# An RWKV block on one core: a small product moves into the duplicate column tile of another

## The chip, the cores and the metric

The kernel runs on one core of a Trainium2 chip. The metric is the device time of one execution in microseconds (us). Engines are named as in the profile: PE is TensorE, DVE is VectorE, ACT is ScalarE, POOL is GpSimd, SP issues most of the DMAs. All data is fp32.

## The reference

The inputs are 8 batches of 256 tokens with 512 channels (32 heads of 16). One batch goes through time mixing and channel mixing:

```
xn = layernorm(x);  sx = shift(xn) - xn
xxx = tanh((xn + sx*maa_x) @ maa_w1)            # 5 parts of 32
x5[g] = xn + sx*(maa_stack[g] + xxx[g] @ maa_w2[g])      # g = 0..4
w = exp(-exp(time_decay + tanh(x5[1] @ decay_w1) @ decay_w2))
r = x5[3] @ Wr.T;  k = x5[0] @ Wk.T;  v = x5[2] @ Wv.T;  g = silu(x5[4] @ Wg.T)
for each token:                                  # s: 16x16 for each head
    a = k (x) v
    out = r . (u*a + s)                          # u = faaaa
    s = a + w*s
x = x + (groupnorm(out) * g) @ Wo.T
xn2 = layernorm(x);  sx2 = shift(xn2) - xn2
x = x + sigmoid((xn2 + sx2*maa_r) @ Wr2.T) * (relu((xn2 + sx2*maa_k) @ Wk2.T)**2 @ Wv2.T)
```

The term `r . (u*a)` is a token's own part: for each head it is the sum over 16 channels of r*k*u, times v. The rest of `out`, `r . s`, is the scan's part.

## The kernel before

Every batch has three stages. `inputs_of_scan` makes the five mixtures x5, the decay w and the projections r, k, v, g. `scan` runs the recurrence: channels lie on partitions, time on the free axis, and for each of 16 pieces of a batch (4 blocks by 4) DVE multiplies by k (the line with `vs`, 128x1024), DVE scans (TENSOR_TENSOR_SCAN, `st`), POOL multiplies by r (`st<-st,r`), and PE gathers four such tiles into a PSUM tile `pat{b}_{blk}` (16 matmuls, 4 column tiles of 32). `rest` does the group norm, the gate, the product with Wo and the channel mixing.

The text names a piece of work by the name of the buffer that it fills, with the batch at the end or in the middle: `psd3` is the decay product of batch 3, `pc3` the own-part product of batch 3, `pat3_0` the gather of its block 0, `psx3` the product with maa_w1, `psm3_1_0` and `psm3_4_0` the products with maa_w2 (each fills four PSUM tiles at once). In the profile all tiles of one pool have one name: every PSUM tile of that pool is `ps`.

- **Decay product `psd`.** Its output has 128 partitions in four column tiles of 32. Tiles 0 and 1 are x5[1] @ decay_w1 (64 columns). Tile 2 is the fifth part of maa_w1, 32 columns, and tile 3 is the same 32 columns again: the array of maa_w1 holds them twice, so that a copy of 64 rows can be taken. ACT then writes tanh of it to `hd` (2 instructions of 64x256) and to `tb` (2 instructions of 64x256), the second four times over the partitions.
- **Own part `pc`.** In `scan`, POOL makes rk = r*k (two tiles of 128x512). PE multiplies it with `hm`, the head mask times faaaa: four matmuls of 256 columns, one in each column tile, into a PSUM tile of its own. ACT copies the sums to all heads' rows (4 copies of 64x256, back into rk). POOL multiplies by v (`att`). DVE later adds each `pat` to `att`, and only then the PSUM tile of that `pat` comes free.
- **Buffers.** PSUM has 8 banks; six are the pool `ps`, two are `wrep`, the expanded decay of a scan. Almost every product of PE needs a tile of `ps` that an ACT or DVE instruction has emptied.
- **Order.** Nothing in the code fixes the order across stages. Every piece of work is an `Op` with a rank out of the table `TURNS`. `Plan.order` always takes the piece with the lowest rank whose inputs are ready, gives it buffers, and sets its start by estimated durations; the pieces are then issued in the order of these starts, and each engine works through its own in order. Stages of three batches overlap: inputs of b+1 and b+2, scan of b, rest of b-1. `Plan.tiles` chooses for a product marked "any" between 128-column weights and four 32-column tiles, after its neighbours. `Plan.tables` puts in the ACT table loads.

Of the kernel before, what the change touches and what calls it, by code (L numbers as in the profile page):

```python
# [68 lines left out]
class Plan:  # L69
# [50 lines left out]
    def stage(self):  # L120
# [6 lines left out]
        677 802 765 774 803 804 821 805 860 824 852 838 1013 770 81 748 784 607 738 881 698 699 767 663 60 619  # L127
        756 91 643 714 124 757 469 782 729,
        30 129 83 79 695 150 166 545 703 460 225 541 73 316 365 644 421 350 761 593 558 731 697 742 665 716 606
        612 758 652 638 45 12 206 135 808 568 845 534 874 634 542 820 145 117 879 485 847 57 560 337 360 834 863  # L130
        781 484 160 48 214 892 822 937 723 271 65 565 897 722 557 100 910 523 945 148 15 134 906 1003 394 935 72
        588 660 954 5 823 944 277 379 562 766 844 9 709 576 976 459 1015 51 143 440 1009 177 1021 477 543 1030
        1052 676 1087,
        797 389 501 402 640 445 437 706 313 559 807 829 239 368 217 893 811 136 119 428 907 688 743 938 627 309
        953 395 29 966 506 848 609 1065 991 510 55 1058 531 299 335 1019 882 586 1026 312 1048 1034 854 888 505
        1000 328 940 696 569 305 372 508 655 653 996 311 259 59 215 154 26 1142 1157 371 1147 867 251 1089 388
        234 752 1088 374 1099 1105 1101 611 794 1094 587 1096 306 308 1053 629 1069 1166 383 1197 1102 273 673
        1146 483 1164 1143 439 1158 191 176 1135,
        826 658 646 426 347 228 900 862 288 626 877 668 38 220 3 977 876 227 231 419 980 983 744 672 997 367 258
        17 1079 675 1167 417 387 903 1185 885 455 615 1172 361 197 252 1168 210 232 331 667 1126 574 399 415  # L140
        1024 1132 650 1 1127 466 205 53 577 1129 662 90 1206 470 185 1232 349 1290 404 561 408 896 1255 359 620
        1229 329 1281 380 1085 423 598 1277 186 585 199 1223 970 1301 324 343 1204 1300 591 1324 1217 409 369
        1293 694 1405 246 528 1323 812 285 1358,
        1309 1265 800 507 911 128 1331 322 97 452 209 297 1365 1007 592 25 1109 1363 1035 656 33 1372 835 63
        1373 211 11 283 1410 537 1422 779 464 799 1431 456 1428 1120 1423 420 639 1477 1424 458 926 178 1447
        1453 1018 921 1203 595 1383 909 1540 1338 174 202 1068 1455 635 1121 836 245 1514 524 1513 310 1600 1344
        1605 1283 853 353 236 1595 1579 115 1345 270 1551 1212 1555 730 1549 1544 1113 1559 512 1416 366 188
        1517 1534 28 1611 1591 321 446 74 509 1492 1618 1023 1678 1601 614 1653,
        1408 1552 654 401 659 95 1473 1371 740 1604 1584 1012 1629 1478 1063 725 451 1631 1494 825 1590 1669 787
        1241 1657 196 1001 495 1682 1709 1729 818 1145 1734 1691 1711 1743 1244 1262 265 575 1738 1392 1014 1719  # L150
        334 1690 1587 597 1039 1038 1326 1421 1377 1548 1457 276 810 1716 1419 737 833 1715 429 1751 354 1760
        1562 1811 1834 1632 1836 949 1772 62 1783 1771 685 1776 161 1082 1803 1258 1493 1762 1286 1800 1327 1280
        1160 341 346 1766 573 54 1780 1795 444 1388 1812 1047 1861 1865 44 1918 67 481 1887,
        1761 518 496 669 631 405 1784 1139 988 1499 1785 390 1842 1348 552 333 162 702 1789 866 1849 1417 1123
        1866 1913 375 1010 318 1937 1961 1900 1173 1298 1978 1152 527 1844 1853 1955 1561 414 1980 975 624 1749
        223 1965 1304 1368 1420 1385 1979 1369 875 1036 1778 1315 832 1908 1261 1443 1097 2015 10 2028 279 2063
        1332 66 2075 1982 2061 1224 93 2008 2039 1948 139 2047 454 2090 2095 2086 1201 1731 2083 1634 2103 1230
        2172 465 138 2014 2084 301 2113 2041 250 2080 300 69 2050 2220 625 2251 2232 149 2257,
        1845 2029 972 427 1184 289 1846 1724 1075 2049 2046 599 2072 1321 1221 579 147 2074 948 116 291 2079 489
        1823 2088 472 1838 292 2112 623 2169 1017 1713 2142 2149 682 1896 1454 2144 1029 947 2163 2102 1895 2140  # L160
        1370 474 2121 1220 1710 1901 2126 1781 1933 1655 2122 887 1098 1585 2128 1723 549 1922 286 2193 212 2192
        636 2217 2227 2001 1464 1639 2162 533 2180 2177 841 2200 31 2210 2000 2105 1699 1998 2207 1091 1538 1756
        1234 323 590 2183 2209 327 2214 2161 233 2023 2230 457 2012 2328 771 2064 2353 2376 2391,
        1985 2093 1033 1395 1027 219 1869 1264 1874 2174 2153 789 2188 1532 1438 487 226 2194 2097 1880 2197
        2199 1912 1660 2233 1977 2032 648 2274 384 2280 412 2065 2256 2286 425 1111 2307 2279 1444 386 2298 2277
# [1017 lines left out]
```

## Time and profile before

| | |
|---|---|
| three runs | 619.63, 620.3, 623.63 us; median 620.3 |
| profiled execution | 621.16 us, its span 619.4 us |
| busy, share of the span | PE 97%, DVE 88%, POOL 86%, ACT 66% |
| granted TensorE clock | 0.999 of full speed |

The span runs from the first to the last instruction; 1.76 us of the profiled execution lie around it. A matmul in the profile is an instruction of half a product (fp32 takes two), and ends are modelled, so successive rows of PE overlap by about 0.2 us: how long PE is taken by a piece is read from the start of its row to the start of the next. On ACT, DVE and POOL the durations are the instructions' own.

### The profile page before, as it was taken

What the parts mean: (1) busy time and instruction counts of PE and PEld (TensorE: products, weight loads), DVE (VectorE), ACT (ScalarE), POOL (GpSimd) and SP (SyncE); (2) the same over time, 40 slices, a digit from 0 to 9 for tenths busy, and PEclk for the clock granted to TensorE, in tenths of its full rate; (3) what the DMA queues carried; (4) which work ended last, traced back from release to release, by engine and by line L of the source; (5) the groups of instructions that cost most, each with busy time, mean ns of one, the idle gap of its engine ahead of it and who ended that gap; (6) DMA issues with size and microseconds to landing.
All of it is one profiled execution on the core that took longest, in us unless ns stands there. A gap on an engine that the chain in (4) does not pass through costs nothing.

```text
span 619.4 us, 17893 instructions
## 1 busy us (share of the span) xinstructions
PE 602.7 (97%) x7490; PEld 342.6 (55%) x7490; DVE 545.3 (88%) x492; ACT 409.7 (66%) x962; POOL 534.4 (86%) x441
## 2 busy tenths in 40 slices
PE   9999999998999999999999999999999999999987
PEld 8665555546634764357453784465744464445454
DVE  5489999999999899898998989999999999995342
ACT  4796368668974788757786787766884387634531
POOL 2789999999999999988999989999997989798030
PEclk9999999999999999999999999999999999999999
DMA  8696766887789676958976695867876697951642
GB/s 286 223 232 166 187 182 172 241 240 201 200 202 258 159 203 180 264 152 236 276 204 207 194 236 155 235 193 204 220 208 192 167 278 206 249 192 51 194 133 83
DMA packets 52497, 124.81 MB, mean 202 GB/s; under 512 B 5696, under 2 KB 11200, under 8 KB 52416
## 3 DMA queue, kind: packets, MB, share of 16 engines
q1 hardware_dynamic: 48048, 119.41, 69.8%
q10 hardware_dynamic: 4368, 4.26, 2.3%
q8 instruction: 59, 0.97, 0.7%
q14 instruction: 22, 0.18, 0.1%
HBM read 115.26 MB, written 8.39 MB: 200 GB/s over the span
## 4 chain that ended last, share of the span: by engine, by line
PE 56%; POOL 15%; DVE 11%; DMA 7%; issue 5%; ACT 5%; ACTq 0%; DVEq 0%; POOLq 0%
PE ps L423 48%; POOL st L957 8%; DMA vs<-vo 5%; DVE st L954 5%; PE ps L965 5%; DVE vs L952 2%; POOL mix L692 2%; POOL mix L778 1%; PE ps L818 1%; PE ps L636 1%; DMA s<-in_state 1%; PE ps L547 1%; POOL vs L949 1%; POOL sx L664 1%; DMA vo<-v 1%
## 5 line engine op out<-in xcount | busy, mean ns | idle before, releaser
L954 DVE TENSOR_TENSOR_SCAN st<-wrep,vs 128x1024 f32<-128x1024 f32 x128 | 289.4, 2279 | 5.9 <-ACT wrep L936 2.6
L957 POOL TENSOR_TENSOR st<-st,r 128x1024 f32<-128x1024 f32 x128 | 254.2, 2004 | 9.6 <-DVE st L954 9.0
L952 DVE TENSOR_TENSOR vs<-vs,ps 128x1024 f32<-128x1024 f32 x122 | 144.2, 1205 | 2.4 <-ACT ps L935 1.9
L423 PE MATMUL ps<-Ws,mix 128*32 128x512 f32 (+3 forms) x872 | 115.7, 586 | 0.7 <-ACT mix L1041 0.7
L423 PEld LDWEIGHTS ps<-Ws,mix 128*32 128x32 f32 (+1 forms) x872 | 38.6, 117 | 64.2 <-issue 57.7
L692 POOL TENSOR_TENSOR mix<-mix,xn 128x512 f32<-128x512 f32 x44 | 48.0, 1103 | 26.0 <-ACT mix L690 24.6
L778 POOL TENSOR_TENSOR mix<-mix,xn 128x512 f32<-128x512 f32 x62 | 66.8, 1099 | 1.6 <-DVE mix L762 1.4
L965 PE MATMUL ps<-st,con 128*32 128x256 f32 x1024 | 61.8, 381 | 0.3 <-DVE x L1031 0.2
L423 PE MATMUL ps<-mix,Wv 128*32 128x256 f32 (+1 forms) x904 | 58.6, 380 | 1.2 <-DVE mix L775 1.1
L423 PE MATMUL ps<-mix,Ws 128*32 128x256 f32 (+1 forms) x736 | 58.0, 380 | 1.3 <-ACT mix L690 0.8
L423 PE MATMUL ps<-mix,Wg 128*32 128x256 f32 (+1 forms) x832 | 58.6, 380 | 0.7 <-POOL mix L806 0.7
L423 PE MATMUL ps<-mix,Wk 128*32 128x256 f32 (+1 forms) x712 | 58.2, 380 | 1.1 <-POOL mix L778 1.0
L423 PE MATMUL ps<-mix,Wr 128*32 128x256 f32 (+1 forms) x808 | 58.5, 380 | 0.0
L423 PE MATMUL ps<-Ws,g 128*32 128x512 f32 (+1 forms) x416 | 56.6, 592 | 0.6 <-DVE mix L801 0.6
L760 ACT ACTIVATE ps<-ps,vec 128x256 f32<-128x256 f32 x112 | 46.9, 445 | 10.8 <-PE ps L423 9.1
L423 PEld LDWEIGHTS ps<-mix,Ws 128*32 128x32 f32 (+1 forms) x736 | 38.6, 121 | 19.1 <-ACT mix L690 1.6
L423 PEld LDWEIGHTS ps<-mix,Wk 128*32 128x32 f32 (+1 forms) x712 | 39.0, 122 | 17.8 <-POOL mix L778 2.4
L423 PEld LDWEIGHTS ps<-mix,Wv 128*32 128x32 f32 (+1 forms) x904 | 35.0, 114 | 22.7 <-DVE mix L775 1.8
L423 PEld LDWEIGHTS ps<-mix,Wg 128*32 128x32 f32 (+1 forms) x832 | 36.5, 116 | 19.8 <-POOL mix L806 1.1
L423 PEld LDWEIGHTS ps<-mix,Wr 128*32 128x32 f32 (+1 forms) x808 | 37.0, 117 | 18.2 <-issue 1.0
L965 PEld LDWEIGHTS ps<-st,con 128*32 128x32 f32 x1024 | 31.6, 110 | 26.1 <-issue 4.7
L1107 ACT ACT_TABLE_LOAD x35 | 44.9, 1283 | 0.6
(134 smaller groups left out, 879.2 us busy)
## 6 DMA issues: line engine op xcount, KB each, us to landing
vs<-vo SPq DMA_DIRECT2D x128, 512.0 KB
Ws<-in_fk SPq DMA_DIRECT2D x16, 512.0 KB
Ws<-in_wo SPq DMA_DIRECT2D x16, 512.0 KB
Ws<-in_fr SPq DMA_DIRECT2D x16, 512.0 KB
Ws<-in_fv SPq DMA_DIRECT2D x16, 512.0 KB
x<-in_x SPq DMA_DIRECT2D x9, 512.0 KB
vo<-v ACTq DMA_DIRECT2D x32, 128.0 KB
out<-o SPq DMA_DIRECT2D x15, 256.0 KB
```

The source lines that it names most:

```text
L423: nc.tensor.matmul(out[i : i + n], lhsT=w[:, i : i + n], rhs=x, start=first, stop=final)
L547: nc.tensor.matmul(ps()[:, 0, :], lhsT=warm[:, 0, 0:P], rhs=warm[:, 0, 0:T], start=True, stop=True)
L636: nc.tensor.transpose(to[:, m, n * P : (n + 1) * P], xh[n]()[:, k * P : (k + 1) * P], idt())
L664: take(512, [sx], [xn], lambda xn=xn, sx=sx, e=nc.vector if quick else nc.gpsimd: e.tensor_tensor(sx(), xn()[:, :, 0:T], xn()[:, :, 1 : T ...
L692: gp(512, t, [t, xn[q]], lambda q=q, t=t: nc.gpsimd.tensor_tensor(t(), t(), xn[q]()[:, :, 1 : T + 1], ALU.add))
L760: act(256, p_, [p_, vec], lambda g=g, q=q, m=m, p_=p_: nc.scalar.activation(p_()[:, m, :], p_()[:, m, :], AF.Identity, bias=col(f"maa_{g}" ...
L778: gp(512, t, [t, xn[q]], lambda q=q, t=t: nc.gpsimd.tensor_tensor(t(), t(), xn[q]()[:, :, 1 : T + 1], ALU.add))
L952: dve(4 * T, [vs], [vs, kp], lambda vs=vs, kp=kp: nc.vector.tensor_tensor(paired(vs()), paired(vs()), doubled(kp()), ALU.mult))
L954: dve(4 * T, [st], [w, vs], lambda w=w, vs=vs, st=st: nc.vector.tensor_tensor_scan(st().rearrange("p n t -> p (n t)"), w().rearrange("p n ...
L957: gp(4 * T, st, [st, r], lambda st=st, r=r: nc.gpsimd.tensor_tensor(paired(st()), paired(st()), doubled(r()), ALU.mult), 1.815)
L965: nc.tensor.matmul(pat()[32 * g : 32 * g + 32, 0, :], lhsT=con()[:, s : s + 32], rhs=done[j]()[:, g, :], start=(j == 0), stop=(j == 3),)
L1107: nc.scalar.preload_act_table_set(op.table)
```

## The change

The second copy of the fifth part is no longer computed. For every batch b after the first, the decay product `psd{b}` computes tiles 0 to 2 as before, and in tile 3 (partitions 96 to 127) the own part's sums of batch b-1: `hm` times rk of b-1. The sums of channel blocks 0 and 1 go to the two halves of psd's own PSUM tile, those of blocks 2 and 3 to a second one, `pc{b-1}`. The product of `pc` by itself is gone for batches 0 to 6; batch 7 has no next batch and keeps it.

Since the sums now lie on 32 partitions, ACT copies them with 8 instructions of 32x256 in place of 4 of 64x256, and `tb` is written with 4 instructions of 32x256 in place of 2. Since psd{b} reads rk of batch b-1, the code of rk moves from `scan` to the end of `inputs_of_scan`, and the stages are written down in another sequence. `psd{b}` now waits for POOL's two rk of batch b-1, and `att` of batch b-1 for psd{b}. All numbers of `TURNS` are new.

```diff
-                    for i in range(0, P, 32):
+                    for i in range(0, P if b == 0 else 96, 32):
                         w, src = (dw1()[:, k, i : i + 32], x5[1]) if i < DEC else (w1()[:, k, P + i - DEC : P + i - 32], xin)
                         nc.tensor.matmul(
                             pd()[i : i + 32, 0, :], lhsT=w, rhs=src[k // 2]()[:, k % 2, :], start=(k == begin), stop=(k == end))
+                    if own:
+                        nc.tensor.matmul(own["pc"][k // 2]()[96:128, k % 2, :], lhsT=hm()[:, k, :],
+                                         rhs=own["rks"][k // 2]()[:, k % 2, :], start=True, stop=True)
...
+            if own:
+                own["pc"] = [pd, new("ps", f"pc{b - 1}")]
+                pe(0.432 * len(ks), own["pc"], [dw1, w1, hm, *ins, *own["rks"]], mm, "columns", [hd, tb])
+                continue
...
-        for rows in (slice(0, 64), slice(64, 128)):
-            act(345, tb, [pd], lambda rows=rows: nc.scalar.activation(tb()[rows, :], pd()[64:128, 0, :], AF.Tanh), "tanh")
+        n = 32 if own else 64
+        for rows in (slice(i, i + n) for i in range(0, P, n)):
+            act(345, tb, [pd], lambda rows=rows: nc.scalar.activation(tb()[rows, :], pd()[64 : 64 + n, 0, :], AF.Tanh), "tanh")
...
-        pe(0.437, [pc], [hm, *rks], mm, "columns")
-        for q in range(NQ):
-            for h in range(0, P, 64):
-                act(350, rks[q], [pc], lambda q=q, h=h: nc.scalar.copy(
-                    rks[q]()[h : h + 64, 0, :], pc()[64 * q : 64 * q + 64, 0, :]))
+        if b == NB - 1:
...
+        else:
+            for q, pc in enumerate(got["pc"]):
+                for h in range(0, P, 32):
+                    act(350, rks[q], [pc], lambda q=q, h=h, pc=pc: nc.scalar.copy(
+                        rks[q]()[h : h + 32, 0, :], pc()[96:128, h // 32 % 2, :]))
...
     TURNS = """
-        677 802 765 774 803 804 821 805 860 824 852 838 1013 770 81 748 784 607 738 881 698 699 767 663 60 619
```

The built programs have these counts: PE 400 pieces of work before and 393 now (the seven products), ACT 914 and 956 (28 more copies, 14 more tanh) with 35 and 31 table loads inside the kernel, DVE 490 and 490, POOL 429 and 429, DMAs 251 and 251 on SP and ACT together.

Three places follow, all around the own part of batch 3. Numbers behind names are those of buffers; lines are those of either program (L910 before is L831 now, L818 is L828, L423 is L432, L917 is L942, L826 is L844, L971 is L996).

PE before, at the own part of batch 3: ps_173 is `pv2`, the variance product of batch 2, ps_174 is `pc3`, ps_172 is `psfk1_1`, a product of the channel mixing of batch 1.

```order
L423 MATMUL ps_172<-mix_118,Ws_165 32x256 x8
L989 MATMUL ps_173<-sq_160,con 32x256 x2
L989 MATMUL ps_173<-sq_159,con 32x256 x2
L910 MATMUL ps_174<-rk_151,hm 32x256 x2
L910 MATMUL ps_174<-rk_152,hm 32x256 x2
L423 MATMUL ps_172<-mix_116,Ws_167 32x256 x8
```

PE now, at the decay product of batch 4: ps_173 is `psd4`, ps_174 is `pc3`, ps_170 ahead of it is a part of v of batch 4.

```order
L432 MATMUL ps_170<-mix_110,Wv_77 32x256 x8
L828 MATMUL ps_173<-mix_114,dw_69 32x256 x2
L828 MATMUL ps_173<-mix_117,mw_66 32x256
L831 MATMUL ps_173<-rk_152,hm 32x256
L828 MATMUL ps_173<-mix_114,dw_69 32x256 x2
L828 MATMUL ps_173<-mix_117,mw_66 32x256
L831 MATMUL ps_173<-rk_152,hm 32x256
L828 MATMUL ps_173<-mix_113,dw_69 32x256 x2
L828 MATMUL ps_173<-mix_119,mw_66 32x256
L831 MATMUL ps_174<-rk_151,hm 32x256
```

The four matmuls of the own part left their place between `pv2` and the channel mixing and stand one by one in the fourth position of each group of the decay product, with gather `pat3_0` far ahead of them and `pat3_1` four products behind.

ACT before, the copies of the own part of batch 3 out of ps_174.

```order
L1107 ACT_TABLE_LOAD
L992 ACTIVATE sq_160<-ps_173,eh 128x256
L917 COPY rk_152<-ps_174 64x256
L917 COPY rk_151<-ps_174 64x256 x2
L917 COPY rk_152<-ps_174 64x256
L1040 ACTIVATE mix_119<-ps_172 128x512
```

ACT now, what empties ps_173 (`psd4` with half of the own part).

```order
L956 DMA vo_144<-v_130 4x32x256
L942 COPY rk_152<-ps_173 32x256 x3
L844 ACTIVATE tb_122<-ps_173 32x256 x2
L942 COPY rk_152<-ps_173 32x256
L844 ACTIVATE tb_122<-ps_173 32x256 x2
L971 COPY vs_148<-s_82 128x4
L582 ACTIVATE xh_87,mv_91<-x_161 128x512
L841 ACTIVATE w_134<-ps_173 64x256 x2
```

ACT now, some rows later, what empties ps_174 (`pc3`, the other half).

```order
L971 COPY vs_147<-s_82 128x4
L942 COPY rk_151<-ps_174 32x256 x2
L867 COPY r_128<-ps_170 128x2x256
L942 COPY rk_151<-ps_174 32x256
L867 COPY r_126<-ps_171 128x2x256
L942 COPY rk_151<-ps_174 32x256
```

Four copies in a row became eight in two lots, among the tanh of the decay and the work of other batches.

DVE before, the first add of a gather of batch 3 (L971, ps_173 is `pat3_0`) among scans (L954) and mixtures (L762).

```order
L954 SCALAR_TENSOR_TENSOR st_153<-wrep_169,vs_146 128x1024
L971 TENSOR_TENSOR att_141<-ps_173,att_141 128x256
L762 TENSOR_TENSOR mix_107<-ps_170,sx_105 128x512
L762 TENSOR_TENSOR mix_111<-ps_175,sx_105 128x512
L954 SCALAR_TENSOR_TENSOR st_154<-wrep_169,vs_145 128x1024
```

DVE now: ps_175 is `pat3_0`, ps_170 is `pat3_1` (L979 are the scans, L977 the products with k, L1056 the residual of batch 2).

```order
L979 SCALAR_TENSOR_TENSOR st_158<-wrep_169,vs_147 128x1024
L1056 TENSOR_TENSOR x_161<-ps_170,x_161 128x512
L977 TENSOR_TENSOR vs_148<-vs_148,ps_172 128x1024
L1056 TENSOR_TENSOR x_161<-ps_171,x_161 128x512
L996 TENSOR_TENSOR att_141<-ps_175,att_141 128x256
L996 TENSOR_TENSOR att_141<-ps_170,att_141 128x256
L979 SCALAR_TENSOR_TENSOR st_153<-wrep_169,vs_146 128x1024
```

The add of the first gather moved back to stand right ahead of that of the second.

## Rows read from the trace of the kernel before

**Rows 1.** Windows: busy time of each engine by stretch, with instruction counts.
```profile
0.00:40.00 40.00, 36.57 (x318) 28.83 (x318) 22.43 (x51) 27.33 (x67) 22.42 (x39) 1.00 0.81 249
40.00:165.00 125.00, 119.73 (x1836) 71.18 (x1840) 121.95 (x96) 87.17 (x204) 124.39 (x91) 1.00 0.74 197
165.00:560.00 395.00, 392.15 (x4996) 213.20 (x4992) 377.29 (x311) 274.09 (x656) 372.25 (x302) 1.00 0.77 210
560.00:619.40 59.40, 54.28 (x348) 29.38 (x340) 23.60 (x37) 21.14 (x37) 15.30 (x12) 0.99 0.38 120
sum 619.40, PE 602.74 PEld 342.58 DVE 545.27 ACT 409.74 POOL 534.37; mean PE 150.69 PEld 85.65 DVE 136.32 ACT 102.43 POOL 133.59
...
600.00:619.40 19.40, 16.01 (x59) 9.63 (x57) 3.33 (x8) 3.43 (x6) 0.00 (x0) 0.97 0.26 83
```

**Rows 2.** The page's chain of work that ended last, shares of the span.
```profile
PE 56%; POOL 15%; DVE 11%; DMA 7%; issue 5%; ACT 5%; ACTq 0%; DVEq 0%; POOLq 0%
```

**Rows 3.** Timeline of PE around `pc2` (start, duration, engine, line).
```profile
184.59 0.61 PE L910 MATMUL ps<-rk,hm 128*32 128x256 f32 x8
185.02 1.91 PE L965 MATMUL ps<-st,con 128*32 128x256 f32 x32
186.74 0.39 PE L818 MATMUL ps<-mix,dw 128*32 128x256 f32 x2
186.76 0.39 PE L818 MATMUL ps<-mix,mw 128*32 128x256 f32 x2
186.96 0.39 PE L818 MATMUL ps<-mix,dw 128*32 128x256 f32 x2
```

**Rows 4.** Timeline of PE around `pc0`, then around `pc1` (in brackets: idle before, releaser).
```profile
55.12 1.20 PE L910 MATMUL ps<-rk,hm 128*32 128x256 f32 x8
56.44 0.93 PE L423 MATMUL ps<-ta,mw2a 32*128 32x256 f32 x12
...
102.61 0.64 PE L910 MATMUL ps<-rk,hm 128*32 128x256 f32 x8 [0.67 <-DVE mix L762]
...
103.21 1.07 PE L423 MATMUL ps<-mix,Wv 128*32 128x256 f32 x16
```

**Rows 5.** Groups by line and form: count, busy us, mean ns, idle before.
```profile
L957 POOL TENSOR_TENSOR st<-st,r 128x1024 f32<-128x1024 f32 x128 | 254.2, 2004 | 9.6 <-DVE st L954 9.0 <-PE ps L423 0.5
L1107 ACT ACT_TABLE_LOAD x35 | 44.9, 1283 | 0.6
L946 ACT COPY vs<-s 128x4 f32<-128x4 f32 x128 | 22.0, 191 | 31.9 <-DMA vs<-vo 27.0 <-ACT v L849 1.8 <-POOL s L898 1.5
L917 ACT COPY rk<-ps 64x256 f32<-64x256 f32 x32 | 11.7, 365 | 2.2 <-PE ps L910 1.2 <-ACT v L849 0.6
L826 ACT ACTIVATE tb<-ps 64x256 f32<-64x256 f32 x16 | 6.1, 380 | 0.3
L867 ACT COPY v<-ps 128x256 f32<-128x256 f32 x2 | 0.7, 361 | 0.2 <-PE ps L423 0.2
```

**Rows 6.** Timeline of PE at `pat0_0`, and of the adds' line L971 what it waited for.
```profile
59.27 1.91 PE L965 MATMUL ps<-st,con 128*32 128x256 f32 x32
...
L971 DVE TENSOR_TENSOR att<-ps,att x32: 397/416/427, 77.0 to 567.9; 128x256 f32<-128x256 f32 x32
...
  POOL att L923: 3.3, 1
```

**Rows 7.** Waits of PE, first and last of seventeen: total us, times, longest.
```profile
PE ps L636 <- ACT xh L616: 1.9, 1, 1.9
...
PE ps L423 <- ACT r L849: 0.5, 1, 0.5
...
PE ps L965 <- DVE x L1031: 0.2, 1, 0.2
```

**Rows 8.** Timeline of PE at `psm5_4_0`.
```profile
373.55 0.71 PE L423 MATMUL ps<-tb,mw2b 32*128 32x256 f32 x8 [0.45 <-ACT r L849]
```

More of the change, by code (lines that the diff above doesn't have):

```diff
@@ L722, in inputs_of_scan @@
     def inputs_of_scan(b, got):
+        own = gots[b - 1] if b else None
         early = [new("mix", f"xin0_{q}") for q in range(NQ)] if b == 0 else None
@@ L879, in inputs_of_scan @@
             act(512, t, [ps], lambda t=t, ps=ps: nc.scalar.activation(t(), ps(), AF.Silu), "silu")
+        got["rks"] = []
+        for q in range(NQ):
+            r, k, rk = got["r", q], got["k", q], new("rk", f"rk{b}_{q}")
+            gp(512, rk, [r, k], lambda rk=rk, r=r, k=k: nc.gpsimd.tensor_tensor(rk(), r(), k(), ALU.mult))
+            got["rks"].append(rk)
     def by_group(t):
@@ L899, in scan, with mm @@
             by_m(s0()), by_m(s0()), two(cm()).unsqueeze(2).to_broadcast([P, 2, S, 2]), ALU.add))
[L902 to L918 removed]
+        atts, rks = [new("att", f"att{b}_{q}") for q in range(NQ)], got["rks"]
+        if b == NB - 1:
+            pc = new("ps", f"pc{b}")
+            def mm():
+                for i in range(NK):
+                    nc.tensor.matmul(
+                        pc()[32 * i : 32 * i + 32, 0, :], lhsT=hm()[:, i, :], rhs=rks[i // 2]()[:, i % 2, :], start=True, stop=True)
+            pe(0.437, [pc], [hm, *rks], mm, "columns")
+            for q in range(NQ):
+                for h in range(0, P, 64):
+                    act(350, rks[q], [pc], lambda q=q, h=h: nc.scalar.copy(
+                        rks[q]()[h : h + 64, 0, :], pc()[64 * q : 64 * q + 64, 0, :]))
+        else:
[3 more added lines that the diff above has]
+                        rks[q]()[h : h + 32, 0, :], pc()[96:128, h // 32 % 2, :]))
         for blk in range(NK):
@@ L1097, in tile_rwkv_block @@
     phases[0].append((0, plan.stage()))
+    gots = [{} for _ in range(NB)]
+    stages = [(inputs_of_scan, 0, 0)]
     for b in range(NB):
-        got = {}
-        for i, stage in enumerate((inputs_of_scan, scan, rest)):
-            stage(b, got)
-            phases[b + i].append((i, plan.stage()))
+        stages += [(inputs_of_scan, 0, b + 1)] * (b + 1 < NB) + [(scan, 1, b), (rest, 2, b)]
+    for stage, i, b in stages:
+        stage(b, gots[b])
+        phases[b + i].append((i, plan.stage()))
     with tc.manual_schedule():
```

10 lines of the change are left out of this document (removed), and 246 rows, old and new, of the table TURNS.

## The prediction

> **What bounds the kernel now.** I read the windows first [rows 1], to see which engine has no room in which stretch. PE is busy for 602.74 of 619.4 us. From 165 to 560 us it is busy for 392.15 of 395: there its queue never runs dry, and 2.85 us are all that better timing could win. From 40 to 165 us it is idle for 5.27 of 125, and POOL is the full engine, 124.39 of 125. At the end 3.39 us follow PE's last matmul (16.01 busy of 19.40). DVE (377.29) and POOL (372.25 of 395) are not far behind PE in the long middle, at 96% and 94%. ACT has the most room, 274.09 of 395. Then the chain that ended last [rows 2]: 56% of it is PE, 15% POOL, 11% DVE. So what leaves PE counts in the middle of the program, and may not in the first quarter. The third view is the timeline of PE around the moved product [rows 3, 4], for what it costs, and the last the groups by line [rows 5], for what ACT is given in exchange.
>
> **The product that leaves.** `pc2` begins at 184.59 us and the next piece at 185.02 [rows 3]: 0.43 us of PE, although its row is 0.61 long, since rows overlap. Five of the seven that go (`pc2` to `pc6`) lie in the stretch where PE is full: 5 x 0.43 = 2.15 us, on the path. The other two, `pc0` and `pc1`, lie in POOL's stretch. They take 56.44 - 55.12 = 1.32 and 103.21 - 102.61 = 0.60 us [rows 4], and before `pc1` PE idled for 0.67. What goes there is worth between nothing (PE then waits for POOL's work instead) and 1.32 + 0.60 + 0.67 = 2.59; I take the two bare products, 0.86, nearer to the lower end, because their excess is waiting that will find another place. Sum: 2.15 + 0.86 = 3.01 us, from 2.15 to 4.74.
>
> **The tile that takes it.** The decay product keeps its number of matmuls; a quarter of them read other weights and other data. Its rows already start in pairs 0.02 us apart, 186.74 and 186.76, and the next pair at 186.96 [rows 3], with two different moving tiles (x5 and the first mixture). `pc` itself runs four column tiles with four different moving tiles, two matmuls each, in its 0.43 us. So a third moving tile should cost nothing. The upper bound is that it does not overlap, and then it costs what `pc` cost, 7 x 0.43 = 3.01, and nothing is won.
>
> **What ACT gets.** 28 more copies and 14 more tanh of 32x256. No row has 32 partitions. The rows on either side of it: 64x256 takes 365 ns as a copy and 380 as tanh, 128x256 takes 361 [rows 5]: the number of partitions makes no difference, so I take 365 and 380, 28 x 0.365 + 14 x 0.380 = 15.5 us. The lower bound is the shortest copy, 191 ns for 128x4, which gives 8.0. Against it stand four fewer table loads in the new order, 4 x 1.283 = 5.1 us. Net 10.4 us (2.9 at the lower bound), on an engine that is idle for 121 of 395 us in the middle: nothing on the path by itself. What hides it is that idle time; without it, 10.4 us would be far more than the gain.
>
> **New waits.** psd{b} waits for POOL's rk of b-1; behind it in PE's queue stands everything, since PE works in order. `att` of b-1 waits for psd{b} and the copies, and behind the adds in DVE's queue stand the scans. POOL's and DVE's work is the same in amount, 429 and 490 pieces, and so are SP's DMAs; the new table only moves them. The new order puts rk eight or more PE pieces ahead of the decay product in three batches, and four ahead of `psd7`. It leaves two PE pieces, some 3.5 us, ahead of `psd1`, `psd4` and `psd5`. I take nothing for it, and 2.00 us each (one of POOL's products with r, 2004 ns [rows 5], in front) as the upper end.
>
> **PSUM.** This is the part that I weigh most. A bank that holds a gather is free only after its add. Counted in the order of issue, between `pat{b}_0` and its add stand 9, 5, 10, 2, 5, 6, 1, 4 pieces of PE before (mean 5.3), and 12, 4, 12, 14, 17, 12, 17, 11 now (12.4): 7 pieces more, of some 1.72 us each (185.02 to 186.74 [rows 3], a gather). The decay product's bank is held for 8.3 pieces in place of 6.3, the second one for 6.6 in place of 4.1. Together a bank out of six is taken for some 20 us more in each batch, and a batch takes about 75. Long holding alone does not stop PE: in batch 0 the gather began at 59.27 and the first add of the whole kernel at 77.0, and one add waited 3.3 us for `att` [rows 6], while no wait of PE is over 1.9 us. But the products of maa_w2 need four banks at once. One of them waited 0.45 us at 373.55 for ACT to empty a bank [rows 8]. I take nothing for it in the forecast, and price it as a rival.
>
> The Trainium skill, in TensorEngine Tiling (Array Packing), section Performance Considerations under PSUM Bottleneck, speaks against this change: column tiling makes PE quicker but not the emptying of PSUM, so the copies can become the limit, and it advises to divide them between ScalarE and VectorE. The change does the reverse, twice the copies, all on ACT. The trace of before is no proof for it, as PE's seventeen waits are 0.2 to 1.9 us each [rows 7] and ACT is idle for a third of the time; if the rule decided here, the time would be that of the first rival.
>
> **The sum.** The profiled execution took 621.16 us, of which 619.4 are the span; less 3.0 gives 618.2. The median of the runs is 620.3, 0.9 below it, and I predict on the median: 620.3 - 3.0 = **617.3 us**, own range 615.0 to 619.6 (the ends of the first term, and about a microsecond for where the waits of a new order fall).
>
> **Rivals.**
>
> 1. *The banks run short; slower.* Each of the seven decay products that carry an own part leaves one bank too few for the maa_w2 product or the projection behind it, and PE waits for ACT or DVE there. A wait costs between 0.45 [rows 8] and 1.9 [rows 7]; 7 x 0.9 = 6.3, the ends 3.2 and 13.3. Time: 617.3 + 6.3 = 623.6, from 620.5 to 630.6. It decides from 0.43 us of new waiting for each batch. For it: first adds 12 pieces behind their gathers, eight copies in two lots. Against it: only 2.85 us of idle in the middle now, with holds as long in batches 0 and 2. The skill's rule above would come out here.
> 2. *POOL is late with rk; slightly slower.* Three places with 2.00 us each: 617.3 + 6.0 = 623.3. Against it: two of the three lie after 165 us, where POOL has 6% to spare.
> 3. *Nothing is won.* Either the fourth tile does not overlap, or DVE and POOL, 96% and 94% busy, set the pace and PE only waits more: 620.3, from 619.6 to 621.5.
> 4. *The new order is better on its own.* All numbers of the table are new, and ACT has four table loads less. Half of the idle time of PE goes: 1.4 of 2.85 in the middle, 2.6 of 5.27 before it, and 0.9 of the 1.73 idle in the last stretch that lie ahead of PE's last matmul (5.12 less 3.39). Time: 617.3 - 4.9 = 612.4, from 611 to 615. Against it: POOL has no room in the stretch where the most would have to be won.
>
> **How the numbers follow.** The forecast has 0.52, nothing won 0.15, the banks 0.14, POOL late 0.04, a better order 0.15. To hold the time 8 times in 10 the range must reach into the better order and well into the banks' case: 612.5 to 624.5. A change of 1%, 614.1 or 626.5 us, is about what a measurement of this kernel can tell from none. Faster by more than that: most of the fourth rival and a little of the forecast's edge, 0.16. Slower: the upper part of the first rival and a little of the second, 0.07. The rest, 0.77, lies within 1%.
>
> **What would show it.** In the profile of the changed kernel, the decay product's 32 instructions should still take 1.72 us from start to start, as the gather does; if 2.1 or more, the fourth tile does not overlap. The group of the old product should be down to 8 instructions. The copies and tanh of 32x256 should show 350 to 390 ns, and ACT some 420 us busy. PE's idle time between 165 and 560 us should stay near 3 us; if it is 6 or more, and the waits are for ACT's copies or DVE's adds, the banks were the matter, and if they stand ahead of the decay product and name POOL's rk, the second rival. If DVE and POOL are busier than now in the middle and PE idles by 3 us more, nothing was won. The prediction is wrong if the idle time at the start or in the last stretch moves by more than 2 us, since no term here speaks for it.

## The result, and the profile after

The changed kernel takes 623.65 us, the median of 20 runs (619.39 to 628.38); the kernel before took 620.7 in 20 runs beside it (619.29 to 624.48). The ratio is 1.0048, with an interval from 1.0027 to 1.007: half a per cent slower, where 3 us less were forecast. Two more series gave 1.0037 (1.0015 to 1.006) and 1.0044 (1.0027 to 1.006). Four executions of the changed kernel were profiled, of 620.46 to 621.6 us, all quicker than its median; the one shown here took 620.46 us, with a span of 618.7. So a profile shows less than what the median loses.

First the windows of that execution (PE, PEld, DVE, ACT, POOL busy with counts, granted clock, DMA share, GB/s), against [rows 1]:

```profile
0.00:40.00 40.00, 36.23 (x342) 28.11 (x342) 24.02 (x51) 23.55 (x57) 20.57 (x37) 1.00 0.73 232
40.00:165.00 125.00, 117.33 (x1709) 76.61 (x1710) 116.76 (x95) 88.32 (x215) 122.29 (x89) 0.99 0.74 194
165.00:560.00 395.00, 391.81 (x4925) 212.99 (x4924) 378.40 (x311) 285.20 (x693) 375.76 (x304) 1.00 0.76 213
560.00:618.70 58.70, 54.97 (x270) 32.60 (x268) 22.91 (x38) 22.36 (x38) 15.13 (x13) 1.00 0.35 121
```

PE is busy for 600.35 us in all, 2.4 less than before: the product did go. PE has 248 matmul instructions fewer than before (7490 and 7242 in all). Only 56 of them are the product's; the other 192 are gone because `Plan.tiles` chooses otherwise in the new order, and e2, where that alone has changed, keeps PE busy as long as before (602.82 us). From 165 to 560 us PE idles for 3.19 (2.85 before). From 40 to 165 it idles for 7.67, against 5.27, and its clock is below 1.00. The other three profiles have 3.59 to 4.78 us and 7.69 to 9.04 for these two stretches.

The chain that ended last, by engine and by line (to be held against [rows 2]):

```profile
PE 69%; DMA 13%; DVE 7%; ACT 4%; issue 2%; POOL 2%; SPq 1%; ACTq 0%; DVEq 0%; POOLq 0%
PE ps L432 60%; DMA vs<-vo 11%; PE ps L990 6%; DVE st L979 4%; DVE vs L977 1%; PE ps L645 1%; DMA vo<-v 1%; PE ps L828 1%; SPq L421 1%; DMA Ws<-in_wv 1%; ACT xn L668 1%; ACT ps L770 1%; PE ps L1014 1%; ACT mix L699 0%; DVE mix L772 0%
```

DMA went from 7% of the chain to 13%, nearly all of it `vs<-vo`: the load that spreads v over the partitions for a scan. PE's timeline at `psd2` (compare [rows 3]; L831 is the own part in the fourth tile, L1014 the piece behind):

```profile
109.85 0.39 PE L828 MATMUL ps<-mix,dw 128*32 128x256 f32 x2
109.86 0.38 PE L828 MATMUL ps<-mix,mw 128*32 128x256 f32 x1
109.87 0.38 PE L831 MATMUL ps<-rk,hm 128*32 128x256 f32 x1
...
111.38 0.38 PE L831 MATMUL ps<-rk,hm 128*32 128x256 f32 x1
111.57 0.81 PE L1014 MATMUL ps<-sq,con 128*32 128x256 f32 x6
```

The three kinds start 0.01 us apart, and from 109.85 to 111.57 pass 1.72 us. The decay product of [rows 3], with two moving tiles, took 1.73 us (186.74 to 188.47): the third moving tile costs nothing. The groups that answer to [rows 5] (count, busy us, mean ns, idle before):

```profile
L1134 ACT ACT_TABLE_LOAD x31 | 39.8, 1283 | 0.5
...
L971 ACT COPY vs<-s 128x4 f32<-128x4 f32 x128 | 23.7, 194 | 48.5 <-DMA vs<-vo 45.7 <-DMA vo<-v 1.2 <-ACT k L867 0.6
...
L942 ACT COPY rk<-ps 32x256 f32<-32x256 f32 x56 | 20.3, 366 | 3.2 <-PE ps L831 1.2 <-DVE vs L977 1.2
...
L844 ACT ACTIVATE tb<-ps 32x256 f32<-32x256 f32 x28 | 10.5, 377 | 0.5
```

Copies and tanh take the time that was forecast for each. The second row stands out. L971 is the copy by which ACT puts the given state into the start column of `vs`, after the DMA has filled the tile. Before (L946) these copies made ACT idle for 27.0 us until a load landed, now for 45.7. The waits, largest of ACT and then those that depend on it (us in total, times, longest):

```profile
ACT vs L971 <- DMA vs<-vo: 45.7, 28, 5.6
...
DVE vs L977 <- ACT vs L971: 10.2, 9, 2.5
...
PE ps L645 <- ACT xh L625: 5.3, 8, 2.3
```

ACT works in order, so what stands behind such a copy waits with it. The scan's product on DVE waits for the copy as well, 10.2 us in nine waits; the waits of DVE before show none of that kind. PE waited once for the normalised x before (1.9 us, [rows 7]), now eight times, 5.3 us in all. The longest, in the timeline of ACT, PE and POOL:

```profile
35.33 1.02 ACT L961 ACTIVATE wrep<-w 128x1020 f32<-128x1020 f32 x1
...
41.12 0.20 ACT L971 COPY vs<-s 128x4 f32<-128x4 f32 x1 [4.76 <-DMA vs<-vo]
41.22 1.51 ACT L625 ACTIVATE xh<-xt,nm,rs 128x512 f32<-128x512 f32 x2
41.39 2.19 POOL L974 TENSOR_TENSOR vs<-vs,k 128x1024 f32<-128x1024 f32 x1 [4.80 <-ACT vs L971]
...
42.08 0.44 PE L645 MATMUL ps<-idt,xh 128*128 128x128 f32 x1 [2.28 <-ACT xh L625]
```

From 36.36 to 41.12 ACT does nothing but wait for a landing; the two `xh` behind the copy need nothing of it. PE stands still until 42.08. The windows right behind show a second effect:

```profile
42.00:46.00 4.00, 3.65 (x13) 3.08 (x14) 2.38 (x2) 2.95 (x9) 4.00 (x3) 0.57 1.05 273
46.00:50.00 4.00, 4.00 (x20) 3.43 (x19) 3.97 (x3) 2.79 (x8) 4.00 (x4) 1.00 1.03 264
```

After the pause the granted clock is 0.57 on average, that is mostly the lower of its two levels (1.2 in place of 2.4 GHz), and full again from 46 us.

### The profile page after: what moved, and what is told of

The parts are those of the page before. It is cut to its first block, busy times and chain, and to the rows that moved or that the text cites. A ratio compares the mean times of both kernels' runs of the same rounds, so it can differ in the third digit from the quotient of the medians.

```text
span 618.7 us, 17422 instructions
## 1 busy us (share of the span) xinstructions
PE 600.4 (97%) x7242; PEld 350.3 (57%) x7242; DVE 542.1 (88%) x492; ACT 419.4 (68%) x1000; POOL 533.7 (86%) x441
## 3 DMA queue, kind: packets, MB, share of 16 engines
q1 hardware_dynamic: 48048, 119.41, 68.6%
## 4 chain that ended last, share of the span: by engine, by line
PE 69%; DMA 13%; DVE 7%; ACT 4%; issue 2%; POOL 2%; SPq 1%; ACTq 0%; DVEq 0%; POOLq 0%
PE ps L432 60%; DMA vs<-vo 11%; PE ps L990 6%; DVE st L979 4%; DVE vs L977 1%; PE ps L645 1%; DMA vo<-v 1%; PE ps L828 1%; SPq L421 1%; DMA Ws<-in_wv 1%; ACT xn L668 1%; ACT ps L770 1%; PE ps L1014 1%; ACT mix L699 0%; DVE mix L772 0%
## 5 line engine op out<-in xcount | busy, mean ns | idle before, releaser
L979 DVE TENSOR_TENSOR_SCAN st<-wrep,vs 128x1024 f32<-128x1024 f32 x128 | 288.6, 2276 | 4.2 <-ACT wrep L961 1.6
L982 POOL TENSOR_TENSOR st<-st,r 128x1024 f32<-128x1024 f32 x128 | 253.8, 2002 | 3.0 <-DVE st L979 2.8
L977 DVE TENSOR_TENSOR vs<-vs,ps 128x1024 f32<-128x1024 f32 x122 | 144.0, 1209 | 11.7 <-ACT vs L971 10.2
L432 PE MATMUL ps<-Ws,mix 128*32 128x512 f32 (+3 forms) x872 | 115.7, 586 | 0.1
L432 PEld LDWEIGHTS ps<-Ws,mix 128*32 128x32 f32 (+1 forms) x872 | 38.1, 116 | 62.5 <-issue 55.5
L432 PE MATMUL ps<-mix,Wv 128*32 128x256 f32 (+1 forms) x856 | 60.1, 380 | 2.3 <-DVE mix L785 1.6
L432 PE MATMUL ps<-mix,Wk 128*32 128x256 f32 (+1 forms) x808 | 59.7, 380 | 1.4 <-ACT xn L668 1.2
L432 PE MATMUL ps<-mix,Wr 128*32 128x256 f32 (+1 forms) x808 | 59.3, 380 | 0.0
L432 PE MATMUL ps<-mix,Wg 128*32 128x256 f32 (+1 forms) x640 | 58.4, 380 | 0.0
L432 PE MATMUL ps<-mix,Ws 128*32 128x256 f32 (+1 forms) x664 | 57.7, 380 | 0.0
L432 PE MATMUL ps<-Ws,g 128*32 128x512 f32 (+1 forms) x440 | 57.2, 592 | 0.1
L971 ACT COPY vs<-s 128x4 f32<-128x4 f32 x128 | 23.7, 194 | 48.5 <-DMA vs<-vo 45.7
L432 PEld LDWEIGHTS ps<-mix,Wv 128*32 128x32 f32 (+1 forms) x856 | 37.0, 115 | 22.9 <-issue 2.5
L432 PEld LDWEIGHTS ps<-mix,Wk 128*32 128x32 f32 (+1 forms) x808 | 38.3, 117 | 19.8 <-issue 1.5
L432 PEld LDWEIGHTS ps<-mix,Ws 128*32 128x32 f32 (+1 forms) x664 | 39.9, 124 | 16.4 <-issue 1.1
L432 PEld LDWEIGHTS ps<-mix,Wg 128*32 128x32 f32 (+1 forms) x640 | 40.5, 126 | 14.9 <-issue 0.7
L432 PEld LDWEIGHTS ps<-mix,Wr 128*32 128x32 f32 (+1 forms) x808 | 38.7, 117 | 17.2 <-issue 0.7
```

The lines of the kernel that those rows point to most:

```text
L432: nc.tensor.matmul(out[i : i + n], lhsT=w[:, i : i + n], rhs=x, start=first, stop=final)
L971: act(4, vs, [s0], lambda j=j, blk=blk, vs=vs: nc.scalar.copy(vs()[:, :, 0:1], s0()[:, blk, 4 * j : 4 * j + 4].rearrange("p (n o) -> p n o ...
L977: dve(4 * T, [vs], [vs, kp], lambda vs=vs, kp=kp: nc.vector.tensor_tensor(paired(vs()), paired(vs()), doubled(kp()), ALU.mult))
L979: dve(4 * T, [st], [w, vs], lambda w=w, vs=vs, st=st: nc.vector.tensor_tensor_scan(st().rearrange("p n t -> p (n t)"), w().rearrange("p n ...
L982: gp(4 * T, st, [st, r], lambda st=st, r=r: nc.gpsimd.tensor_tensor(paired(st()), paired(st()), doubled(r()), ALU.mult), 1.815)
```

## The experiments

The theories at the start: **O**, the new order costs time of its own (first suspected: the stall at 40 us), and **B**, the first rival of the prediction, banks that run short. From the fourth kernel on, **S**: ACT's queue is held up at many places by start-column copies that wait for landings; its rival **D**: the landing itself is late for DVE, and the copy only shows it. All times are medians; "before" is the kernel before on the same chip in the same series.

| kernel | us (runs) | before | ratio, interval |
|---|---|---|---|
| e1: move in the old order | 695.4 (5) | 621.08 | 1.1206 (1.1179 to 1.1233) |
| e2: new order, no move | 622.9 (12) | 621.08 | 1.0034 (1.0015 to 1.0052) |
| e3: after, one copy later | 624.27 (7) | 621.08 | 1.0057 (1.0036 to 1.0078) |
| e4: after, copies away | 618.4 (9) | 620.89 | 0.9952 (0.9934 to 0.9969) |
| e5: e2, copies away | 619.6 (12) | 620.89 | 0.998 (0.9966 to 0.9993) |
| e6: before, copies away | 622.0 (12) | 620.89 | 1.0018 (1.0004 to 1.0032) |
| after in that series | 622.43 (12) | 620.89 | 1.0037 (1.0015 to 1.006) |
| e7: after, all copies later | 625.26 (10) | 620.82 | 1.007 (1.0046 to 1.0094) |
| e8: after, loads past the start column | 621.28 (12) | 620.82 | 1.0013 (0.9994 to 1.0032) |
| e9: e4, 14 of 56 own copies | 617.39 (6) | 620.82 | 0.9931 (0.9915 to 0.9948) |
| e10: e4, no rk in psd | 618.52 (12) | 620.82 | 0.9963 (0.9948 to 0.9979) |
| e11: after, 36 loads past the start | 620.15 (12) | 621.08 | 0.999 (0.9973 to 1.0007) |
| e12: e2, the same 36 loads | 619.86 (12) | 621.08 | 0.9989 (0.9971 to 1.0008) |
| after in that series | 623.96 (6) | 621.08 | 1.0044 (1.0027 to 1.006) |
| e13: e4, 112 own copies | 625.56 (6) | 620.95 | 1.0075 (1.0051 to 1.0099) |
| e4 again, 56 own copies | 618.88 (8) | 620.95 | 0.9961 (0.9945 to 0.9977) |
| e9 again, 14 own copies | 617.36 (6) | 620.95 | 0.9939 (0.9918 to 0.996) |

**The two halves of the change, e1 and e2.** e1 has the code of the change and the old numbers, e2 the code of before and the new numbers, with `pc` right ahead of the decay product.

```diff
     TURNS = """                                # e1, code of after
-        7 30 12 31 34 109 36 16 70 33 67 122
+        680 809 769 778 810 811 830 812 870 833 862 847
     TURNS = """                                # e2, code of before
-        677 802 765 774 803 804 821 805 860 824 852 838
+        7 30 12 31 34 109 36 16 70 33 67 122
```

> The own part in the decay product's fourth tile, but with the ranks of the old table: every piece that both kernels have keeps its old rank, the additional copies and tanh take that of their neighbours, and the decay product of b is allowed to start when its inputs are there (PE keeps 383 of 393 pieces in the old sequence, DVE 481 of 490). Order theory (the new table costs what the move wins): about 617.7 us, 3 below the kernel before. Banks theory (the move itself costs, by PSUM tiles held until the late copies and adds): 621 us or more, with more idle time of PE between 165 and 560 us.

> The kernel before with the ranks of the new table: the own product stays a product by itself, right ahead of the decay product of the next batch, with 4 copies of 64 rows; PE, DVE, POOL and the DMAs keep the sequence of the changed kernel exactly. Order theory: about 626.7 us (623.7 and the 3.0 us of the seven products), with the same idle time of PE near 40 us and a half clock behind it. Banks theory: 620 to 622 us.

e1 took 695.4 us. Its waits name the cause (L817, L928, L934, L982 and L968 there are L831, L942, L948, L996 and L982 of the changed kernel):

```profile
DVE att L982 <- POOL att L934: 37.6, 7, 11.1
POOL st L968 <- DVE st L965: 34.7, 20, 10.4
...
ACT rk L928 <- PE ps L817: 20.4, 5, 8.7
...
POOL att L934 <- ACT rk L928: 17.4, 6, 5.9
```

This is the new wait of `att` in the change: the products `att` of a batch wait for the next batch's decay product, DVE's first add waits for `att`, once in each of seven batches, and the scans wait behind it in DVE's queue. POOL's wait for scans rises from 9.0 us [rows 5] to 34.7. PE's own waits in e1 come from many sides (the largest, 9.8 us in two waits, for a mixture on DVE), and its granted clock is 0.96 in the mean, so not all of the 74 us can be put down to this one chain. The move does not go into the old order as it stands; no third order was tried. The new order alone, e2, costs 1.8 us, and the move on top of it gains nothing. e2's row is that of the changed kernel, with the copies' waits still longer:

```profile
ACT vs L941 <- DMA vs<-vo: 53.5, 28, 6.8
```

**One copy behind xh, e3.** ACT's queue at 40 us, all else in its place:

```diff
-COPY vs_147<-s_83 128x4
 ACTIVATE xh_87<-xt_86,nm_97,rs_95 128x512
 ACTIVATE xh_88<-xt_86,nm_97,rs_95 128x512
+COPY vs_147<-s_83 128x4
```

> The changed kernel with one ACT instruction moved: the start-column copy for the fourth scan tile of block 1 in batch 0 goes from ahead of the two normalisations of batch 2 to right behind them; every other sequence is the same. Order theory: PE's wait of 2.3 us near 40 us goes, and with it the stretch of half clock behind it; 620 to 621.5 us, and less scatter. Banks theory: no change, 623.7 us.

It took 624.27. The stall at 40 us is gone, but its profiled execution, 626.43 us, has another one. In the timeline, here first its rows (L957 is L971, L611 and L631 are L625 and L645), then those of the changed kernel at the same place of the program.

```profile
368.79 0.20 ACT L957 COPY vs<-s 128x4 f32<-128x4 f32 x1 [3.06 <-DMA vs<-vo]
...
373.53 0.33 PE L631 MATMUL ps<-idt,xh 128*128 128x128 f32 x1 [2.41 <-ACT xh L611]
```

```profile
367.10 0.20 ACT L971 COPY vs<-s 128x4 f32<-128x4 f32 x1 [1.08 <-DMA vs<-vo]
...
371.74 0.33 PE L645 MATMUL ps<-idt,xh 128*128 128x128 f32 x1 [0.58 <-ACT xh L625]
```

And the window behind, of e3 and then of the changed kernel (the third number from the end is the clock):

```profile
374.00:378.00 4.00, 3.77 (x13) 3.25 (x14) 3.90 (x4) 4.00 (x11) 1.60 (x3) 0.57 0.53 147
```

```profile
374.00:378.00 4.00, 4.00 (x38) 2.96 (x40) 3.93 (x2) 3.97 (x10) 3.49 (x4) 1.00 0.53 148
```

The order is the same, the loads were issued at the same time, one landing came 1.7 us later: PE waits 1.8 us longer, and the clock falls to 0.57. So theory O in its first form, one bad place, fell: with that place mended another long wait came, behind another copy. That the copies' waits cost time at many places is theory S. The stall at 40 us came again in the other three profiled executions of the changed kernel, with waits of PE of 1.93, 2.12 and 1.45 us. One of these is the single execution below; it took 620.7 us, less than expected.

> The changed kernel once more, for a second profile, since its times scatter from 619.4 to 628.4 us and its one profile is of a quick run (620.5). Both theories: 622 to 626 us. Order theory: more idle time of PE before 165 us than the first profile, or a longer stretch of half clock. Banks theory: more idle time between 165 and 560 us.

**The copies sent away, e4 to e6.** The same edit in the changed kernel, in e2 and in before, with the changed kernel beside them:

```diff
                 act(4, vs, [s0], lambda j=j, blk=blk, vs=vs: nc.scalar.copy(
-                    vs()[:, :, 0:1], s0()[...
+                    away[:].rearrange("p (n o) -> p n o", o=1), s0()[...
```

> The changed kernel, except that ACT's 128 copies of the start column of a scan write to a small tile that nobody reads, not into vs: the state given at the start is left out of the computation. Every engine keeps its instructions and their order, but none of these copies waits for the DMA that fills vs; DVE's product waits for that DMA itself. Theory S (ACT's queue: in the new order these copies wait 45.7 us for DMA landings, and what stands behind them, the normalised x and the emptying of PSUM, comes late to PE, at another place in each run, with a half-clock stretch behind each longer stall): about 617.5 us (616.5 to 619), a granted clock of 1.0 in most runs, and a scatter of 3 us in place of 9. Theory B (PSUM banks held longer, or the order itself): 623.0, from 622 to 624.5, scatter as before. Theory D (the DMA landing is late for DVE's product and scan, and the copy only shows it): 621.5 or more.

> The new order without the move (the own part's product by itself, right ahead of the decay product), with the same edit of the start-column copies: the given state is left out. Theory S: 620.5 us (619.5 to 621.5), 3.0 more than with the move, since the product's 7 x 0.43 us are then all that differs. Theory B: 622.9 as with the copies in place, and within 1 us of the changed kernel with the same edit. Theory D: 621 or more.

> The kernel before with the same edit of the start-column copies: the given state is left out. Theory S: its copies wait 27.0 us in all, but little that PE needs stands behind them: 619.8 us (619 to 620.5), at most 1 us less than with the copies in place. Theories B and D: 620.3 to 621.0, no difference.

> The changed kernel as it is, beside the three others on one chip. All theories: 623.5 us (622.5 to 624.5), with runs from 619.5 to 628.

The changed kernel falls from 622.43 to 618.4 us, the new order without the move from 622.9 (in its own series) to 619.6, and the runs of e4 spread over 3.6 us in place of 7.2. So most of S holds, and D falls: DVE's products still wait for the loads themselves, 6.6 us in five waits, and the time falls all the same. Two things came out otherwise than S had them. The granted clock is 1.0 in one run of e4 out of nine and 0.997 in the other eight, where the changed kernel beside it has 1.0 in five of twelve: the stretches at the lower clock did not go, and the 4 us were not won there. And before does not gain but lose, 1.1 us; why was not tried. The edit takes two waits away at once, that of ACT's queue for the landing and that of DVE's product for the copy; it does not tell one from the other. In e4 the copies' row reads

```profile
L971 ACT COPY away<-s 128x4 f32<-128x4 f32 x128 | 24.2, 189 | 3.9 <-DMA vo<-v 2.0 <-ACT v L867 1.2
```

and twice a PSUM tile is what PE waits for, as rival 1 had it. Here is the longer one, the longest wait of PE in e4: the tile of the product with Wr is free after ACT's copy of k, and that copy stands behind a mixture that waits for POOL's sx.

```profile
48.86 0.51 ACT L699 ACTIVATE mix<-sx,vec 128x256 f32<-128x256 f32 x1 [4.30 <-POOL sx L673]
...
49.59 0.59 ACT L867 COPY k<-ps 128x512 f32<-128x512 f32 x1 [0.22 <-DMA Wg<-in_wg]
...
50.22 5.35 PE L432 MATMUL ps<-mix,Wr 128*32 128x256 f32 x64 [3.20 <-ACT k L867]
```

From 52 to 54 us the granted clock is 0.50. e5, without the move, has the same wait (3.5 us), so it belongs to the new order: with the copies out of the way, another instruction in ACT's queue holds PE up. The second wait is that of a maa_w2 product for the add of a gather (L996):

```profile
378.82 0.40 DVE L996 TENSOR_TENSOR att<-ps,att 128x256 f32<-128x256 f32 x1
...
379.28 0.71 PE L432 MATMUL ps<-tb,mw2b 32*128 32x256 f32 x8 [1.95 <-DVE att L996]
```

**Two complete versions, e7 and e8.**

```diff
-        done.sort(key=lambda op: op.start)                                                    # e7
+        late = lambda op: max(op.start, min(op.start + 2.0, op.after[0].start - 0.6)) if op.engine == "ACT" and op.bufs[0].pool == "vs" else op.start
+        done.sort(key=late)
-    "(h g) t -> h (g t)", g=4) ... lambda vs=vs: vs().rearrange("p g t -> p (g t)")           # e8
+    "(h g) t -> h g t", g=4)[:, :, 1:T] ... lambda vs=vs: vs()[:, :, 1:T]
```

> The changed kernel, complete: in the finished order each of ACT's 128 start-column copies is put up to 2.0 us later by the plan's own times, but ahead of its product; every other instruction of every engine keeps its place. Theory S (the copies hold up ACT's queue while they wait for DMA landings): the 45.7 us of waiting fall to about half, and the time to 619.5 us (618 to 621), between 623 and the 618.4 without any such wait. Theory D (only the landing of the data matters): 622 or more, since DVE's products get their copies later still.

> The changed kernel, complete, in its own order: the DMA that fills vs leaves the start column out (four runs of 1020 bytes for each partition in place of one of 4096), so that ACT's copy of the start column need not wait for it. Theory S: 618.4 us, as with the copies sent away, if the transfer takes no longer in shorter runs; DMA queues are 70% busy here, so if it does take longer, the products on DVE wait for it: 621 to 625. Theory B or D: 622 or more in any case.

e7 was a miss for S: the waits fell to 27.3 us, where about half of 45.7 was expected, yet the time is 625.26, and 622 or more was D's forecast. Its profiled execution is its slowest (630.4 us):

```profile
219.90 0.20 ACT L971 COPY vs<-s 128x4 f32<-128x4 f32 x1 [4.20 <-DMA vs<-vo]
...
220.13 1.22 DVE L977 TENSOR_TENSOR vs<-vs,ps 128x1024 f32<-128x1024 f32 x1 [3.24 <-ACT vs L971]
...
221.16 2.05 PE L432 MATMUL ps<-mix,Wk 128*128 128x256 f32 x4 [2.49 <-ACT xn L668]
221.19 1.04 POOL L673 TENSOR_TENSOR sx<-xn 128x512 f32<-128x512 f32 x1 [4.03 <-ACT xn L668]
```

The copy passed some work and now stands ahead of other work, the `xn` that PE and POOL wait for, and closer to the product that waits for it: DVE's waits for copies rise from 10.2 us to 21.9. So a late landing reaches the other engines by two ways, through ACT's queue and through DVE's product, and e7 traded one for the other; this way of moving the copies found no better place. In e8 the copies no longer need the load, and 621.28 is less than the changed kernel's 622.4 to 624.0 in other series (the intervals of the ratios overlap), but not 618.4. Its packets take more of the queue's time; DMA queue of e8, then of the changed kernel in its execution of 621.6 us (packets, MB, share of 16 engines):

```profile
q1 hardware_dynamic: 97200, 119.14, 74.2%
```

```profile
q1 hardware_dynamic: 48048, 119.41, 69.0%
```

The first profile of the changed kernel has 68.6%, e4's 69.7%. That this is what e8 lacks is argued, not shown; the wait for k of e4 stands in its profile too, with 4.2 us.

**Only the loads that were waited for, e11 and e12.** e8's edit for 36 of the 128 loads, with and without the move.

```diff
+    PAST = "000 001 011 013 020 032 102 132 133 202 ...".split()
+                split = 1 if f"{b}{blk}{j}" in PAST else 0
-                ... .rearrange("(h g) t -> h (g t)", g=4) ...
+                ... .rearrange("(h g) t -> h g t", g=4)[:, :, split:T] ...
```

> The changed kernel, complete, in its own order: 36 of the 128 loads of vs, those whose start-column copy was seen to wait for the landing, leave the start column out (runs of 1020 bytes), the other 92 stay as they are. If the wait of ACT's queue for landings is what the changed kernel loses: 618.8 us (617.5 to 620), between e4's 618.4 and e8's 621.3, and with it below the kernel before (620.8). If e4 gained only because the state was left out, or short runs cost as much as the wait: 621.3 to 623.

> The new order without the move, complete, with the same 36 loads. Theory S: 620.0 us (619 to 621.2), 1.2 to 2 more than with the move, as between e5 (619.6) and e4 (618.4). Otherwise 622 to 623, as without the edit.

> The changed kernel as it is, beside the two others on one chip: 623.0 us (622 to 624).

e11 takes 620.15 us, 3.8 less than the changed kernel beside it, and the intervals of the ratios do not meet. So the copies' dependence on the landing costs that much in a complete kernel as well. Some copies still wait, 12.5 us in all in its profiled execution (623.29 us, its slowest). There DVE's products wait 13.1 us for loads and copies, no less than the 10.2 of the changed kernel, which speaks for ACT's queue as the way on which most is lost; no run takes only one of the two waits away. e11 and e12 are the quickest complete versions found, 0.9 and 1.2 us below before, and neither interval excludes no difference. Where 1.2 to 2 us for the move were expected, the time with it (620.15) and without it (619.86) is the same.

**What eats the rest, e9, e10 and e13.** With the copies sent away the move is worth 1.2 us (e5 to e4; the intervals overlap a little), not 3.0. That the product was sized rightly a place in e5 shows, where it still stands by itself:

```profile
197.20 0.61 PE L905 MATMUL ps<-rk,hm 128*32 128x256 f32 x8
197.63 0.39 PE L813 MATMUL ps<-mix,dw 128*32 128x256 f32 x2
```

```diff
-    act(350, rks[q], [pc], lambda q=q, h=h, pc=pc: nc.scalar.copy(rks[q]()[h : h + 32, 0, :], pc()[...]))
+    act(350, rks[q], [pc], (...) if h // 32 % 4 == 3 else (lambda: None))                     # e9
+    act(350, rks[q], [pc], lambda q=q, h=h, pc=pc: [nc.scalar.copy(...) for _ in range(2)])   # e13
-    rhs=own["rks"][k // 2]()[:, k % 2, :]                                                     # e10
+    rhs=x5[1][k // 2]()[:, k % 2, :]
```

> The kernel of e4 (start-column copies sent away), and of the 56 copies of the own part's sums 42 left out, so that most of the own part is wrong in the output: ACT has 15 us less to do in the places where the two banks are emptied. If ACT's additional work and the longer holding of banks eat what is missing of the product's 3.0 us (1.2 are seen between e5 and e4): 616.6 us (616 to 617.3). If DVE and POOL set the pace there, or POOL's rk does: 618.4 (617.7 to 619.2).

> The kernel of e4 (start-column copies sent away), and the own part's matmuls in the decay product read the second mixture, which the decay product reads anyway, in place of POOL's rk: the own part is wrong in the output, and PE no longer waits for POOL there. If the wait for rk eats the rest of the 3.0 us: 616.6 us (616 to 617.3). Otherwise 618.4 (617.7 to 619.2).

> The kernel of e4 (start-column copies sent away, so the given state is left out), with each of the 56 copies of the own part's sums made twice: ACT gets 20.5 us more (56 x 0.366) and both banks and the products att come free later. If ACT's additional work in the places where the banks are emptied is what eats the product's 3.0 us: 619.9 us or more (e9, with 42 copies fewer, was 1.0 below e4). If not: 618.4 (617.7 to 619.0), as e4.

> The kernel of e4 once more (the given state is left out), beside the two others on one chip: 618.4 us (617.8 to 619).

> The kernel of e9 once more (given state and 42 of 56 own-part copies left out), on the same chip: if the copies count, 617.3 us and 1.0 below e4; if they do not, the same as e4 within 0.5 us.

POOL's rk is not it: 618.52 against 618.4. More copies do cost time, by e13 clearly: 14, 56 and 112 of them give 617.36, 618.88 and 625.56 us on one chip. The 56 that e13 adds cost 6.7 us (20.5 us of ACT). The 42 that e9 leaves out (15 us of ACT) are worth some 1.5 us, or 1.1 against e10 in the first series; the intervals overlap in the one and touch in the other, so this part is likely and not shown. PE's waits in e13 name the copies, 3.7 us in all, which no wait of PE in e4's profile does:

```profile
PE ps L432 <- ACT rk L942: 2.5, 3, 1.1
...
PE ps L990 <- ACT rk L942: 1.2, 1, 1.2
```

## Why the prediction was wrong

- **The product that leaves, 3.01 us: right as far as seen.** PE is busy for 602.3 to 602.8 us in the profiles with the product by itself (before, e2, e5, e6, e12) and for 599.1 to 600.8 in the four of the changed kernel, some 2.4 less; the product takes 0.43 us in the place of e5 that is shown.
- **The tile that takes it: right.** 1.72 us, as forecast.
- **What ACT gets: right in amount, wrong in what it costs.** 366 and 377 ns, and 419.4 us busy where some 420 were expected. "Nothing on the path by itself", hidden by ACT's idle time, failed: in the places where they stand, 56 such copies more cost 6.7 us (e13), and 42 fewer gave some 1.5, which is not clear of the noise. Idle time of an engine that works in order covers nothing if it lies elsewhere.
- **New waits, taken as nothing.** The wait for rk is nothing (e10). The wait of `att` leads the waits of e1, where the move in the old order costs 74 us.
- **The sum, "about a microsecond for where the waits of a new order fall": the step that failed most.** The new order alone costs 1.8 us (e2), and the start-column copies' wait for landings costs the changed kernel 3.8 to 4.0 (after against e11, and against e4), of the 6.35 us between 617.3 and 623.65. The row was on record: 27.0 us of ACT idle before these copies [rows 5], read there only for the shortest copy's duration. In the new order it is 42.8 to 48.2 us in the four profiles of the changed kernel and 53.5 in e2, and `xh`, the emptying of PSUM and DVE's products stand behind it.
- **Rival 1, banks short: 623.6 by forecast, 623.65 measured, a match by luck.** PE idles for 3.19 to 4.78 us in the middle in the four profiles, where it asked for 6 or more, and what decides is a wait for a DMA. Only with that wait gone do banks show, in waits of 3.20 and 1.95 us and in the series of own copies. The Trainium skill's rule (TensorEngine Tiling (Array Packing), section Performance Considerations, PSUM Bottleneck: the copies out of PSUM can become the limit) agrees with that series, by e13's 6.7 us for twice the copies; it is not what decides here.
- **Rival 2, POOL late: excluded by e10**, in the kernel without the copies' waits. **Rival 3, nothing won:** so it came out with e11 and e12. Of its two reasons the first is excluded, as the fourth tile overlaps; that DVE and POOL set the pace was not tried by itself.
- **Rival 4, a better order: hidden.** With the copies sent away the new order is 1.3 us below before as it was (e5 619.6, before 620.89), and 2.4 below before with the same edit (e6 622.0).
- **The prediction's own sign came.** It called itself wrong if the idle time at the start moved by more than 2 us: from 40 to 165 us it rose by 2.40, and by 2.42 to 3.77 in the other profiles.

That e9, with the copies' waits and most of the own copies gone, takes the forecast 617.3 (617.4 us) is in part chance: it makes 14 own copies where before made 28 in these batches, and of its 3.4 us below before, 1.3 come without the move (e5). What stays open: why before is slower with its copies away (e6); how much of the landings' cost goes through ACT's queue and how much through DVE's product; and how the remaining 1 to 2 us divide between ACT's time and the longer holding of banks, which e9 and e13 change together.

## What to carry to other kernels

An engine with a third of its time idle is not free: ask what stands first in its queue, and what stands behind that. An instruction that waits for a DMA landing makes everything behind it on its engine depend on that landing, so look for waits on DMA on engines that empty PSUM or feed TensorE, and take the dependence away (here: a load that leaves out the column that another engine writes, for the loads that were waited for) before tuning the order around it. When a new order comes with a change, time the order without the change.

## What the runs showed of the hardware

After waits of PE of 1.93, 2.12, 2.28 and 2.41 us (three profiles of the changed kernel at 40 us, and e3) a window of 2 us behind shows a granted clock of 0.50 to 0.55, about the lower of the two levels. After waits of 0.58 us, of 1.45 at 40 us in the fourth profile, and of 1.95 in e4 at 379 us it stayed at 1.00. With the 128 loads of 512 KB in runs of 1020 bytes in place of 4096 the queue's packets took 74.2% of the span in place of 68.6 and 69.0, for the same 119 MB. A copy of 32x256 took 366 ns on ACT, as one of 64x256 did (365): half the partitions, no shorter.
